# A graph transformer layer pair on one core: edges in 105 chunks instead of 106, with each border chosen in a scan

## The chip, the cores and the metric

The kernel runs on one core of one Trainium2 chip. A core has TensorE (PE in the profile, with its weight loads as PEld), VectorE (DVE), ScalarE (ACT), GpSimd (POOL) and SyncE (SP), each with its own queue of instructions, and 16 DMA engines that all queues share. The metric is the time on the device in microseconds (us) of one execution; lower is better.

## The reference, cut to what matters

There are 6250 nodes with 128 features and 106250 directed edges, sorted by destination. Two transformer convolutions with two heads follow one another; between them stand a batch normalisation and a ReLU, and behind them a residual and a layer normalisation. The edge features are 64 given numbers and 32 cosines of a time difference.

```python
def _transformer_conv(h, edge_attr, src, dst, Wq, bq, Wk, bk, Wv, bv, We, Ws, bs):
    n = h.shape[0]
    C = Wq.shape[1] // H
    q = (h @ Wq + bq).reshape(n, H, C)
    k = (h @ Wk + bk).reshape(n, H, C)
    v = (h @ Wv + bv).reshape(n, H, C)
    e = (edge_attr @ We).reshape(-1, H, C)
    kj = k[src] + e
    alpha = jnp.einsum('ehc,ehc->eh', q[dst], kj) / jnp.sqrt(jnp.asarray(C, h.dtype))
    amax = jax.lax.stop_gradient(jax.ops.segment_max(alpha, dst, num_segments=n))
    ex = jnp.exp(alpha - amax[dst])
    den = jax.ops.segment_sum(ex, dst, num_segments=n)
    a = ex / den[dst]
    out = jax.ops.segment_sum((v[src] + e) * a[:, :, None], dst, num_segments=n)
    return out.reshape(n, H * C) + h @ Ws + bs
...
h = _transformer_conv(x, edge_attr, src, dst, Wq1, bq1, Wk1, bk1, Wv1, bv1, We1, Ws1, bs1)
mu = h.mean(axis=0)
var = ((h - mu) ** 2).mean(axis=0)
h = (h - mu) / jnp.sqrt(var + 1e-05) * bn_g + bn_b
h = jax.nn.relu(h)
return _transformer_conv(h, edge_attr, src, dst, Wq2, bq2, Wk2, bk2, Wv2, bv2, We2, Ws2, bs2)
...
x = _layernorm(x + _L0_gnn_ref(...), axis=-1, eps=1e-05)
```

The sum over a destination's edges runs over neighbouring edges, since the destinations are sorted. So a chunk of edges that begins at a node's first edge and ends behind a node's last edge can be worked on alone.

## The kernel before

**Chunks.** The edges are cut into `NC` = 106 chunks (L48). Each chunk has room for `CE` = 1024 edges (8 columns of 128) and for `NN` = 64 nodes, whose two heads fill 128 rows. A chunk always works on 1024 edges from its first edge on; edges that belong to the next chunk's nodes are masked out by a code of bits for each node.

**The plan ahead of the layers** (`tile_gnn_resnorm`, from L1154). The borders depend on the data, so the kernel works them out on the core. A border is wanted about every `step` = 1003 edges. For each of the 105 inner borders a window of 128 destinations is loaded (`win`, L1157 to L1160). The window's last destination is the border's node; counting how often it stands in the window (`cnt`, L1208) gives that node's first edge (`first`, L1210). A matmul with ones (L1217) turns the 105 rows into one row with all the nodes and one with all the edges (`both`). From it come `slots`, the first edge of each chunk capped at E - 1024 (L1222), and `at` (L1227), by which three indirect DMAs on POOL load the chunks' sources, destinations and weights as rows (L1231). Then `ends`, `nbs` and `sls` hold the borders for the layers (L1235 to L1237). Some small operations check that no chunk has over 64 nodes or 1024 edges, that two neighbouring chunks span no more than 127 nodes, and that the data is sorted (L1246 to L1257 and L1286 to L1291). The result is `oki` (L1310). With `oki` = 1 the path `ordered` runs, and otherwise a general path that makes no use of the order (L1316 to L1319).

Between these steps, in an order written out by hand, the plan also copies the features and times into the table `xv_d` that the first layer gathers from (`pass_features`, L525 to L532), multiplies the weight matrices together (`matrices`), makes the first block of the table of queries (`tables`, L629 to L635), and turns the loaded rows into columns (`columns`, L1268 to L1275).

**The layers** (`conv`, L701, run twice). The loop runs over rounds k from -4 to `NC` + 2. In round k, chunk k + 4 is fetched (SP loads, and 8 gathers of 128 rows each on POOL, L751), chunk k + 1 is turned by PE (L805) and copied by ACT (L812), chunk k is scored (L830, L831) and put through the exponential, chunk k - 1's weights are turned (L855) and its sums gathered (L862), and chunk k - 2 is divided (`fa`, L870), multiplied with the value matrices and finished. All of it is one order written by hand, and each engine takes its part in that order. In the rounds one step of other work is pulled as well (two in the first four rounds and after round 96): in the first layer the tables of the later blocks and then the passing of finished rows, in the second the tables of the second layer. In the second layer finished chunks are normalised in groups whose starts are `STARTS` (L59), the last groups being short.

In the first layer the cosines of the first 43 chunks are taken one chunk at a time, those of later chunks two at a time (`encode` and `sine`, L760 to L784).

Of the kernel before, what the change touches and what calls it, by code (L numbers as in the profile page):

```python
# [7 lines left out]
F32 = mybir.dt.float32  # L8
I32 = mybir.dt.int32
AF = mybir.ActivationFunctionType  # L10
OP = mybir.AluOpType
AX = mybir.AxisListType

P = 128
# [30 lines left out]
T = 8  # L45
CE = T * P
NN = P // H
NC = 106  # L48
EW = ED + 1

BITS = 8
EC = ED + 2 * BITS
# [3 lines left out]
HIGHEST = 2.0 ** 119  # L56

LG = 10
STARTS = (*range(0, 91, LG), 97, 101, 103, 104, 105)  # L59


@with_exitstack
# [472 lines left out]
def room(nc, pl, const, c, w, brief=None):  # L535
# [9 lines left out]

    return ((wq, w["Wq"]), (wk, w["Wk"]), (web[P - EW:P - 1], w["We"]), (bq, w["bq"].rearrange("(p a) -> p a", a=1)),
            (bk, w["bk"].rearrange("(p a) -> p a", a=1)), (web[P - 1:], w["bv"].rearrange("(a d) -> a d", a=1)),
# [28 lines left out]
def matrices(nc, pl, c, const, bank, brief=None):  # L576
# [3 lines left out]
    for i, w in enumerate((wq, wk, web)):  # L580
# [5 lines left out]
        else:  # L586
            nc.vector.memset(t, 0.0)
            nc.vector.tensor_copy(t[:, :ED], pt[:, P - EW:P - 1])
            nc.vector.tensor_copy(t[:, ED:EW], bk)
        turned.append(t)  # L590
# [72 lines left out]
def ordered(ctx: ExitStack, tc: tile.TileContext, pl, x, dst, edge_attr_64, conv2, bn_g, bn_b, out):  # L663
# [16 lines left out]

    enc_d = dram.tile([NC, P, T * TD], F32, name="enc_d")
    et_d = dram.tile([NC, EC, CE], F32, name="et_d")
    xT = pl.xT = const.tile([P, NP], F32, name="fxT")
# [3 lines left out]
    def first(k):  # L687
        return max(0, N - NN * (NC - k)), min(N - 1 if k == NC - 1 else N - NN, NN * k)

# [11 lines left out]
    def conv(c, extra, first_blocks=None):  # L701
# [20 lines left out]
        def fetch(k):  # L722
# [7 lines left out]
            if c:  # L730
                nc.vector.memset(f[:, :, D + EW:1 + D + EW], 1.0)
            else:
                bits = small.tile([P, T, BITS], I32, name="fbits")
                nc.vector.tensor_tensor(bits, pl.dsts[:, :, k:k + 1].to_broadcast([P, T, BITS]),
                                        pl.bitm[:, None, :].to_broadcast([P, T, BITS]), OP.bitwise_and)
                nc.vector.tensor_scalar(f[:, :, D + EW:D + EW + BITS], bits, 0.0, None, op0=OP.is_equal)
                nc.vector.tensor_copy(f[:, :, D + EW + BITS:], bits)
            s.tab = load.tile([P, NN * H, 3 - c], F32, name="ftab")
# [162 lines left out]
        def finish(k):  # L901
# [10 lines left out]

            k0 = max(i for i in STARTS if i <= k)
            g = k - k0
            n = next(i for i in (*STARTS, NC) if i > k) - k0
            if g == 0:
# [17 lines left out]
        def store(j, at, rows, scale):  # L934
            o = small.tile([NN, D], F32, name="fout")
            nc.scalar.activation(o, rows, AF.Copy, scale=scale)
            if j < NC - 1:
                nc.sync.dma_start(out[bass.ds(at, NN), :], o)
            if j > NC - 3:
                nc.sync.dma_start(tail_d[bass.ds(at - base, NN), :], o)  # L940
# [199 lines left out]
def tile_gnn_resnorm(ctx: ExitStack, tc: tile.TileContext, x, src, dst, edge_attr_64, edge_weight, node_vec,  # L1140
                     time_w, time_b, conv1, conv2, bn_g, bn_b, out):
    nc = tc.nc
    N = x.shape[0]
    E = src.shape[0]
    step = -(-E // NC)
# [4 lines left out]
    nbs = keep.tile([1, NC], I32, name="nbs")  # L1150
# [3 lines left out]
    with tc.tile_pool(name="plan", bufs=1) as pl, tc.tile_pool(name="planw", bufs=2) as mw, \  # L1154
            tc.tile_pool(name="planp", bufs=2, space=bass.MemoryType.PSUM) as pp, tc.manual_schedule():
        R = NC - 1
        win = pl.tile([R, P], I32, name="win")  # L1157
        for r0, r1 in ((0, R // 16 * 16), (R // 16 * 16, R)):
            nc.sync.dma_start(win[r0:r1], bass.AP(tensor=dst.tensor, offset=dst.offset + step * (r0 + 1) - (P - 1),
                                                  ap=[[step, r1 - r0], [1, P]]))  # L1160
        NP = got.NP = -(-(N + NN) // GE) * GE
        got.hT = keep.tile([P, NP], F32, name="fhT")
# [21 lines left out]
        tau_i = pl.tile([P, 1], I32, name="tau_i")  # L1184
# [5 lines left out]
        nxt = pl.tile([P, NC], F32, name="nxt")  # L1190
# [3 lines left out]
        ends = pl.tile([1, 2, NC + 1], F32, name="ends")  # L1194
# [9 lines left out]
        winf = pl.tile([R, P], F32, name="winf")  # L1204
        nc.vector.tensor_copy(winf, win)
        eqw = pl.tile([R, P], F32, name="eqw")
        cnt = pl.tile([R, 1], F32, name="cnt")
        nc.vector.tensor_scalar(eqw, winf, winf[:, P - 1:], None, op0=OP.is_equal, op1=OP.add, accum_out=cnt)  # L1208
        first = pl.tile([R, 1], F32, name="first")
        nc.vector.tensor_scalar(first, cnt, -1.0, 1.0, op0=OP.mult, op1=OP.add)  # L1210
        nc.vector.tensor_add(first, first, tau_i[:R])

        vals = pl.tile([R, 2, NC], F32, name="vals")
        nc.vector.tensor_scalar(vals[:, 0], nxt[:R], winf[:, P - 1:], None, op0=OP.mult)
        nc.vector.tensor_scalar(vals[:, 1], nxt[:R], first, None, op0=OP.mult)
        both = pp.tile([P, 2, NC], F32, name="both", tag="fpx")
        nc.tensor.matmul(both, ones[:R], vals, start=True, stop=True)  # L1217

        NR = -(-NC // 16) * 16
        slots = pl.tile([1, NR], F32, name="slots")  # L1220
        nc.vector.memset(slots, 0.0)
        nc.vector.tensor_scalar(slots[:, :NC], both[0:1, 1], float(E - CE), None, op0=OP.min)  # L1222

        pi = pp.tile([P, 1], F32, name="pi", tag="one", bufs=1)
        at = pl.tile([P, 1], I32, name="at")
# [3 lines left out]
        for flat, dtype in ((src, I32), (dst, I32), (edge_weight, F32)):  # L1229
# [2 lines left out]
                out=t.rearrange("c t p -> c (t p)"), out_offset=None, in_=flat.rearrange("(e a) -> e a", a=1),  # L1232
                in_offset=bass.IndirectOffsetOnAxis(ap=at[:NR], axis=0))
            flats.append(t)
        nc.vector.tensor_copy(nbs, both[0:1, 0])  # L1235
        nc.vector.tensor_copy(ends[:, :, :NC], both[0:1])
        nc.vector.tensor_copy(sls, slots[:, :NC])  # L1237

        def bank():
# [46 lines left out]
        nc.vector.tensor_tensor(down, alld[:, 1:ww], alld[:, :ww - 1], OP.is_lt)  # L1286
        worst = pl.tile([P, 1], F32, name="worst")
        nc.vector.tensor_reduce(worst, down, AX.X, OP.add)
        full = pl.tile([R, 1], F32, name="full")
        nc.vector.tensor_scalar(full, cnt, float(P) - 0.5, None, op0=OP.is_gt)  # L1290
        nc.vector.tensor_add(worst[:R], worst[:R], full)  # L1291
        next(passed)
        first_table = tables(nc, got, 0, xT0, 0, mw, wide)
        next(first_table)
# [32 lines left out]
def launch_program(arrays):  # L1327
    import numpy as np
    import concourse.bacc as bacc

    nc = bacc.Bacc("TRN2", target_bir_lowering=False, num_devices=1)
    given, args = {}, {}
    for name, a in arrays.items():
        a = np.ascontiguousarray(a)
        given[f"in_{name}"] = a
        args[name] = nc.dram_tensor(f"in_{name}", a.shape, mybir.dt.from_np(a.dtype), kind="ExternalInput").ap()
    out = nc.dram_tensor("out_0", arrays["x"].shape, F32, kind="ExternalOutput").ap()
    convs = [{w: args[f"{_PRE}{w}{c}"] for w in _WEIGHTS} for c in (1, 2)]
    with tile.TileContext(nc) as tc:
        tile_gnn_resnorm(tc, *(args[n] for n in ("x", "src", "dst", "edge_attr_64", "edge_weight", "node_vec")),  # L1340
                         args[_PRE + "time_w"], args[_PRE + "time_b"], *convs, args[_PRE + "bn_g"],
                         args[_PRE + "bn_b"], out)
    return nc, given
# [7 lines left out]
```

## Time and profile before

| what | value |
|---|---|
| runs of the kernel | 2757.98, 2755.56, 2752.11 us; median 2755.56 |
| the profiled execution's own time | 2730.3 us |
| its span, first to last instruction | 2728.4 us |
| mean granted TensorE clock | 0.952 |
| plan ahead of the layers | about 39 us, to the first gather at 38.71 |
| first layer, first to last `fa` | 125.0 to 1381.8 us |
| second layer, from its second `fa` to its last | 1491.9 to 2715.6 us |

Rows of the groups view read: line, engine and operation, tile written and tiles read, shapes and count, then busy time in us and the mean of one in ns, then the idle time of that engine right before these instructions and what ended it. Rows of the timeline read: start in us, duration in us, engine, line, operation, and in square brackets the idle time before it with what ended it. Rows that show only the `fa` line read: durations min/median/max in ns, then the start of the first and of the last in us. PE's ends are modelled, so its busy share is not a share of its peak.

### The profile page before, as it was taken

To read this page: it belongs to the slowest core of one execution; us is meant where nothing else is said; L and a number is where in the kernel's file an instruction comes from. 1 tells how busy PE (TensorE), PEld (TensorE's weight loads), DVE (VectorE), ACT (ScalarE), POOL (GpSimd) and SP (SyncE) were. 2 spreads that over 40 slices of the span, in tenths; PEclk is the share of its full clock that TensorE was granted. 3 is DMA by queue.
4 is the path that set the end of the run, shared out by engine and by line. 5 is a ranking of instruction groups with operands and counts; after the bars stand their busy time and mean duration, and the time that the engine had idled before them with its cause. 6 is when DMAs were issued, how large, how long until landed. Compare 5 with 4: busy or idle time off the path is not lost. (4 is left out here: it accounts for less than half of the span.)

```text
span 2728.4 us, 39114 instructions
## 1 busy us (share of the span) xinstructions
PE 2340.9 (86%) x11586; PEld 1725.5 (63%) x11586; DVE 1342.3 (49%) x4162; ACT 1241.6 (46%) x2167; POOL 1619.5 (59%) x1717
## 2 busy tenths in 40 slices
PE   5599999999898989888957998888898888888887
PEld 3366666767676767666734665666666666666655
DVE  5366666666666666666634333333333333333333
ACT  2366666665555555445522343333334333333344
POOL 3466666566666666666335666666666666666660
PEclk7799999999999999999978999998999999999998
DMA  6255555545555455555436554555555555544440
GB/s 205 80 177 145 154 164 149 150 131 161 160 151 158 130 163 154 142 150 149 119 106 175 157 154 144 147 156 155 152 153 142 159 151 152 156 135 129 137 135 27
DMA packets 241161, 396.59 MB, mean 145 GB/s; under 512 B 62609, under 2 KB 158094, under 8 KB 237614
## 3 DMA queue, kind: packets, MB, share of 16 engines
q1 hardware_dynamic: 167728, 239.73, 29.5%
q0 software_dynamic: 54656, 113.07, 16.2%
q10 hardware_dynamic: 18558, 41.20, 4.3%
q8 instruction: 98, 1.61, 0.2%
q14 instruction: 121, 0.99, 0.1%
HBM read 277.19 MB, written 113.17 MB: 143 GB/s over the span
## 5 line engine op out<-in xcount | busy, mean ns | idle before, releaser
L751 POOL DMA_INDIRECT ff<-xv_d,fsrcs x848 | 810.1, 955 | 512.8 <-issue 213.0
L751 POOL DMA_INDIRECT ff<-hn_d,fsrcs x824 | 782.2, 949 | 458.8 <-issue 208.7
L812 ACT COPY fft<-fpx 128x512 f32<-128x512 f32 x418 | 246.1, 589 | 1150.2 <-remote 439.9
L862 PE MATMUL fpa<-ff,fpt 128*128 128x225 f32 x3392 | 684.2, 354 | 0.6 <-issue 0.6
L862 PEld LDWEIGHTS fpa<-ff,fpt 128*128 128x128 f32 x3392 | 628.6, 190 | 4.8 <-issue 1.3
L830 PE MATMUL fps<-fft,ftab 128*128 128x512 f32 x848 | 480.4, 650 | 65.5 <-ACT fft L812 45.8
L837 DVE TENSOR_REDUCE flow<-fps 128x1 f32<-128x512 f32 x424 | 285.4, 686 | 455.5 <-PE fpx L805 124.5
L855 PEld LDWEIGHTS fppt<-fident,fs 128*128 128x128 f32 x1696 | 203.4, 145 | 145.2 <-issue 76.4
L856 ACT COPY fpt<-fppt 128x512 f32<-128x512 f32 x424 | 229.4, 585 | 108.8 <-PE fppt L855 47.5
L845 ACT ACTIVATE fs<-fps,fm 128x512 f32<-128x512 f32 x424 | 269.1, 689 | 4.8 <-DVE fm L839 2.1
L805 PE MATMUL fpx<-fident,ff 128*128 128x128 f32 x1696 | 259.3, 276 | 5.3 <-issue 1.1
L830 PEld LDWEIGHTS fps<-fft,ftab 128*128 128x128 f32 x848 | 168.0, 233 | 126.6 <-ACT fft L812 68.2
L855 PE MATMUL fppt<-fident,fs 128*128 128x128 f32 x1696 | 234.6, 282 | 11.6 <-ACT fft L810 5.4
L831 PE MATMUL fps<-fxT,ftab 112*128 112x512 f32 x424 | 236.8, 642 | 2.8 <-DMA fxT<-et_d 2.8
L831 PE MATMUL fps<-fet,ftab 112*128 112x512 f32 x424 | 221.0, 603 | 11.2 <-issue 11.2
L805 PEld LDWEIGHTS fpx<-fident,ff 128*128 128x128 f32 x1696 | 203.4, 142 | 34.8 <-issue 22.7
L817 PE MATMUL fpe<-fident,ff 128*112 128x128 f32 x848 | 133.4, 281 | 72.6 <-ACT fft L812 69.7
L831 PEld LDWEIGHTS fps<-fet,ftab 112*128 112x128 f32 x424 | 106.8, 252 | 91.0 <-issue 88.9
L831 PEld LDWEIGHTS fps<-fxT,ftab 112*128 112x128 f32 x424 | 90.7, 214 | 116.3 <-issue 111.0
L885 DVE COPY fat<-fpo 128x256 f32<-128x256 f32 x212 | 89.2, 421 | 138.9 <-remote 58.9
L817 PEld LDWEIGHTS fpe<-fident,ff 128*112 128x112 f32 x848 | 95.8, 136 | 88.9 <-ACT fft L812 83.3
L818 ACT COPY fet<-fpe 112x512 f32<-112x512 f32 x212 | 127.4, 601 | 45.1 <-remote 16.0
(203 smaller groups left out, 2402.4 us busy)
## 6 DMA issues: line engine op xcount, KB each, us to landing
fmsg<-in_edge_attr SPq DMA_DIRECT2D x212, 256.0 KB
et_d<-fet SPq DMA_DIRECT2D x106, 448.0 KB
fxT<-et_d SPq DMA_DIRECT2D x106, 448.0 KB
ftab<-tab_d SPq DMA_DIRECT2D x106, 192.0 KB
tab_d<-fo ACTq DMA_DIRECT2D x13, 1536.0 KB
ff<-xv_d,fsrcs POOLq DMA_INDIRECT x848
enc_d<-fzs SPq DMA_DIRECT2D x106, 128.0 KB
ftab<-tab_d SPq DMA_DIRECT2D x106, 128.0 KB
```

The source lines that it names most:

```text
L751: nc.gpsimd.indirect_dma_start(out=f[:, t, (1 if c else 0):1 + D], out_offset=None, in_=(h_d if k < RAW else hn_d) if c else pl.xv_d, in_o ...
L805: turn = nc.tensor.transpose(px[:, t * P:(t + 1) * P], s.f[:, u * 4 + t, 1:1 + D], ident)
L812: nc.scalar.copy(s.ft[:, u * GE:(u + 1) * GE], px)
L817: nc.tensor.transpose(pe[:EC, t * P:(t + 1) * P], s.f[:, u * 4 + t, 1 + D:], ident)
L818: nc.scalar.copy(s.et[:, u * GE:(u + 1) * GE], pe[:EC])
L830: nc.tensor.matmul(ps, s.tab[:, :, 0], s.ft[:, w], start=True, stop=False)
L831: nc.tensor.matmul(ps, s.tab[:EC, :, 1], s.et[:, w], start=False, stop=True)
L837: nc.vector.tensor_reduce(low[:, u:u + 1], s.ps[u], AX.X, OP.min)
L845: nc.scalar.activation(s.s[:, u * GE:(u + 1) * GE], s.ps[u], AF.Exp, bias=s.bias, scale=-1.0)
L855: nc.tensor.transpose(pp[:, t * P:(t + 1) * P], s.s[:, at:at + P], ident)
L856: nc.scalar.copy(s.pt[:, u * GE:(u + 1) * GE], pp)
L862: nc.tensor.matmul(s.pa, s.pt[:, t * P:(t + 1) * P], s.f[:, t, 1:1 + D + EW], start=t == 0, stop=t == T - 1)
```

## The change

`NC` becomes 105, so a border is wanted every 1012 edges. The window of 128 destinations now lies around the border's place (`MID` = 63 in front). Two counts replace the one: how often the middle destination stands at or in front of the middle, and how often at or behind it. The first gives the node's first edge (`down_`), the second the next node's first edge (`up`). Of these two places one is taken for each border, in order: the later one (`up`) where the chunk that ends there still has no more than 1024 edges and 64 nodes, and otherwise the earlier one. Whether it does depends on how the border before was chosen, so there are two answers for each border, and a scan along the row (`tensor_tensor_scan`) carries the choice from one to the next (`later`). The chosen edge and node then go where the one place went before, and the check on the windows looks at both counts.

```diff
-NC = 106
+NC = 105
 EW = ED + 1
+MID = P // 2 - 1
...
-STARTS = (*range(0, 91, LG), 97, 101, 103, 104, 105)
+STARTS = (*range(0, 91, LG), 96, 100, 102, 103, 104)
...
-            nc.sync.dma_start(win[r0:r1], bass.AP(tensor=dst.tensor, offset=dst.offset + step * (r0 + 1) - (P - 1),
+            nc.sync.dma_start(win[r0:r1], bass.AP(tensor=dst.tensor, offset=dst.offset + step * (r0 + 1) - MID,
...
-        cnt = pl.tile([R, 1], F32, name="cnt")
-        nc.vector.tensor_scalar(eqw, winf, winf[:, P - 1:], None, op0=OP.is_equal, op1=OP.add, accum_out=cnt)
-        first = pl.tile([R, 1], F32, name="first")
-        nc.vector.tensor_scalar(first, cnt, -1.0, 1.0, op0=OP.mult, op1=OP.add)
-        nc.vector.tensor_add(first, first, tau_i[:R])
-
-        vals = pl.tile([R, 2, NC], F32, name="vals")
-        nc.vector.tensor_scalar(vals[:, 0], nxt[:R], winf[:, P - 1:], None, op0=OP.mult)
-        nc.vector.tensor_scalar(vals[:, 1], nxt[:R], first, None, op0=OP.mult)
-        both = pp.tile([P, 2, NC], F32, name="both", tag="fpx")
+        cnt = pl.tile([R, 2], F32, name="cnt")
+        for i, w in enumerate((slice(0, MID + 1), slice(MID, P))):
+            nc.vector.tensor_scalar(eqw[:, w], winf[:, w], winf[:, MID:MID + 1], None, op0=OP.is_equal, op1=OP.add,
+                                    accum_out=cnt[:, i:i + 1])
+        edge = pl.tile([R, 2], F32, name="edge")
+        nc.vector.tensor_scalar(edge[:, 0:1], cnt[:, 0:1], -1.0, 1.0, op0=OP.mult, op1=OP.add)
+        nc.vector.tensor_copy(edge[:, 1:], cnt[:, 1:])
+        nc.vector.tensor_tensor(edge, edge, tau_i[:R].to_broadcast([R, 2]), OP.add)
+
+        vals = pl.tile([R, 3, NC], F32, name="vals")
+        nc.vector.tensor_scalar(vals[:, 0], nxt[:R], edge[:, 0:1], None, op0=OP.mult)
+        nc.vector.tensor_scalar(vals[:, 1], nxt[:R], edge[:, 1:], None, op0=OP.mult)
+        nc.vector.tensor_scalar(vals[:, 2], nxt[:R], winf[:, MID:MID + 1], None, op0=OP.mult)
+        both = pp.tile([P, 3, NC], F32, name="both", tag="fpx")
         nc.tensor.matmul(both, ones[:R], vals, start=True, stop=True)
+
+        cut = pl.tile([1, 3, NC], F32, name="cut")
+        nc.vector.tensor_copy(cut, both[0:1])
+        down_, up, node = (cut[:, i] for i in range(3))
+        reach = pl.tile([1, 2, NC], F32, name="reach")
+        near = pl.tile([1, 2, NC], F32, name="near")
+        nc.vector.memset(reach[:, :, 0:1], 0.0)
+        for i, (since, n) in enumerate(((up, NN), (down_, NN - 1))):
+            nc.vector.scalar_tensor_tensor(reach[:, i, 1:], since[:, :NC - 1], float(CE), up[:, 1:], op0=OP.add,
+                                           op1=OP.is_ge)
+            nc.vector.scalar_tensor_tensor(near[:, i, 1:], node[:, :NC - 1], float(n), node[:, 1:], op0=OP.add,
+                                           op1=OP.is_ge)
+        nc.vector.tensor_mul(reach[:, :, 1:], reach[:, :, 1:], near[:, :, 1:])
+        nc.vector.tensor_sub(reach[:, 0], reach[:, 0], reach[:, 1])
+        later = pl.tile([1, NC], F32, name="later")
+        nc.vector.tensor_tensor_scan(later, reach[:, 0], reach[:, 1], 0.0, OP.mult, OP.add)
+        nc.vector.tensor_sub(up, up, down_)
+        nc.vector.tensor_mul(up, up, later)
+        nc.vector.tensor_add(ends[:, 1, :NC], down_, up)
...
-        nc.vector.tensor_scalar(slots[:, :NC], both[0:1, 1], float(E - CE), None, op0=OP.min)
+        nc.vector.tensor_scalar(slots[:, :NC], ends[:, 1, :NC], float(E - CE), None, op0=OP.min)
...
-        nc.vector.tensor_copy(nbs, both[0:1, 0])
-        nc.vector.tensor_copy(ends[:, :, :NC], both[0:1])
+        nc.vector.tensor_add(ends[:, 0, :NC], node, later)
+        nc.vector.tensor_copy(nbs, ends[:, 0, :NC])
         nc.vector.tensor_copy(sls, slots[:, :NC])
...
-        full = pl.tile([R, 1], F32, name="full")
-        nc.vector.tensor_scalar(full, cnt, float(P) - 0.5, None, op0=OP.is_gt)
-        nc.vector.tensor_add(worst[:R], worst[:R], full)
+        full = pl.tile([R, 2], F32, name="full")
+        most = pl.tile([R, 2], F32, name="most")
+        nc.vector.memset(most[:, 0:1], float(MID + 1))
+        nc.vector.memset(most[:, 1:], float(P - MID))
+        nc.vector.tensor_tensor(full, cnt, most, OP.is_ge)
+        for i in range(2):
+            nc.vector.tensor_add(worst[:R], worst[:R], full[:, i:i + 1])
```

## The prediction

> **What bounds the kernel now.** I read the page's summary first, then the groups of instructions by line, then two views cut by time: the busy time of the engines by stretch, and the instructions that write the tile `fa`, of which there is exactly one per chunk and layer.
>
> ```profile
> PE 2340.9 (86%) x11586; PEld 1725.5 (63%) x11586; DVE 1342.3 (49%) x4162; ACT 1241.6 (46%) x2167; POOL 1619.5 (59%) x1717
> ```
>
> ```profile
> L751 POOL DMA_INDIRECT ff<-xv_d,fsrcs x848 | 810.1, 955 | 512.8 <-issue 213.0 <-PE fpa L862 130.5 <-PE fpx L805 101.4
> L862 PE MATMUL fpa<-ff,fpt 128*128 128x225 f32 x3392 | 684.2, 354 | 0.6 <-issue 0.6
> L812 ACT COPY fft<-fpx 128x512 f32<-128x512 f32 x418 | 246.1, 589 | 1150.2 <-remote 439.9 <-PE fpx L805 340.4 <-PE fpo L899 195.5
> ```
>
> TensorE (PE) is the busiest engine. Of the idle time before ScalarE's largest group (L812), 340.4 + 195.5 us ended at a named PE instruction; the gathers on POOL, when not spaced by issue (213.0 us), waited mostly for PE too. So a chunk is paced by PE first, with POOL (8 gathers x 955 ns and 213.0 / 848 = 0.25 us of issue each, 9.6 us) not far behind. Which of the two it is matters little here, since all their large groups have counts in proportion to chunks: 3392 = 16 x 2 layers x 106, 848 = 8 x 106. A chunk less takes one round from each layer whichever engine sets the pace. The question is what a round is worth:
>
> ```profile
> L870 DVE TENSOR_SCALAR fa<-fpa,finv x72: 452/453/455, 125.0 to 990.2; 128x225 f32<-128x225 f32 x72
> L870 DVE TENSOR_SCALAR fa<-fpa,finv x23: 452/453/455, 1063.9 to 1326.6; 128x225 f32<-128x225 f32 x23
> L870 DVE TENSOR_SCALAR fa<-fpa,finv x7: 452/453/454, 1326.6 to 1381.8; 128x225 f32<-128x225 f32 x7
> L870 DVE TENSOR_SCALAR fa<-fpa,finv x77: 452/453/455, 1491.9 to 2393.7; 128x225 f32<-128x225 f32 x77
> L870 DVE TENSOR_SCALAR fa<-fpa,finv x21: 452/453/454, 2404.9 to 2643.1; 128x225 f32<-128x225 f32 x21
> L870 DVE TENSOR_SCALAR fa<-fpa,finv x7: 452/453/454, 2654.9 to 2715.6; 128x225 f32<-128x225 f32 x7
> ```
>
> Dividing each stretch by its count less one gives 12.19 and 11.94 us a round in the first layer, 11.87 and 11.91 in the second; the last six intervals, where gathers have run out, are 9.20 and 10.12. The other work spread over the rounds (tables of the next blocks, one step a round) is a fixed 84 steps; with two steps in each of the first four rounds it is used up at round 79, so the stretches from 1063.9 and from 2404.9 are rounds without it.
>
> **The change part by part.** *One round less in each layer.* The last groups' starts, the windows' place and the row counts change no instruction's number. The total of table steps, row writes and group ends (15 `STARTS` groups before and after) stays, and so does the fast end of each layer. What goes is a plain round: 11.94 + 11.91 = 23.85 us. In it are its 16 gathers, 7 SP loads and its stores. From chunk 43 the encodings share one sine by pairs: 63 chunks left one alone, 62 leave none, so one ScalarE sine and its table load go too, inside that price. Lower bound: only the end's rounds are saved, 9.20 + 10.12 = 19.32. Upper bound: rounds with table work, 12.19 + 11.91 = 24.1.
>
> *The borders, ahead of the layers.* These rows are all on DVE, except the matmuls (PE), DMA issue (SP) and gather (POOL):
>
> ```profile
> 3.55 0.35 DVE L1208 TENSOR_SCALAR_CACHE_REDUCE eqw<-winf 105x128 f32<-105x128 f32 x1
> 3.82 0.08 DVE L1208 DVE_READ_ACCUMULATOR eqw<-winf 105x1 f32 x1
> 3.94 0.15 DVE L1210 TENSOR_SCALAR first<-cnt 105x1 f32<-105x1 f32 x1
> 4.27 0.27 DVE L1214 TENSOR_SCALAR vals<-nxt,winf 105x106 f32<-105x106 f32 x1
> 4.46 0.27 DVE L1215 TENSOR_SCALAR vals<-nxt,first 105x106 f32<-105x106 f32 x1
> 4.78 1.07 PE L1217 MATMUL both<-vals,pones 105*128 105x212 f32 x2 [4.78 <-DVE vals L1215]
> 5.89 0.26 DVE L1222 TENSOR_SCALAR slots<-both 1x106 f32<-1x106 f32 x1 [1.06 <-PE both L1217]
> 6.77 0.16 DVE L1227 CAST at<-pi 112x1 int32<-112x1 f32 x1 [0.62 <-PE pi L1226]
> 7.02 0.36 DVE L1236 COPY ends<-both 1x212 f32<-1x212 f32 x1
> 7.43 0.36 DVE L1247 TENSOR_TENSOR span<-ends 1x212 f32<-1x212 f32 x1
> 7.82 0.20 DVE L1248 TENSOR_SCALAR span<-span 1x106 f32<-1x106 f32 x1
> 8.64 0.27 DVE L1255 TENSOR_TENSOR two<-ends 1x105 f32<-1x105 f32 x1
> 8.94 0.20 DVE L1256 TENSOR_SCALAR two<-two 1x105 f32<-1x105 f32 x1
> 9.17 0.25 DVE L1257 TENSOR_REDUCE bad<-two 1x1 f32<-1x105 f32 x1
> 10.46 0.34 DVE L525 COPY fxrows<-fnv 128x48 f32<-128x48 f32 x1 [1.03 <-DMA fnv<-in_node_vec]
> 20.53 0.16 DVE L1291 TENSOR_TENSOR worst<-worst,full 105x1 f32<-105x1 f32 x1
> 24.01 2.32 DVE L635 SCALAR_TENSOR_TENSOR fo<-fpx,fb,fcode 128x512 f32<-128x512 f32 x2 [2.46 <-PE fpx L629]
> 26.16 0.69 DVE L1268 CAST rowf<-rows 106x1024 f32<-106x1024 int32 x1
> 29.68 0.14 DVE L1310 TENSOR_SCALAR oki<-tot 1x1 int32<-1x1 f32 x1
> 31.34 0.32 SPq L529 DMA_DIRECT2D xv_d<-fxrows  x1
> 38.71 0.96 POOL L751 DMA_INDIRECT ff<-xv_d,fsrcs  x1 [27.93 <-DVE fbits L734]
> ```
>
> A step's price is the distance from its start to the next one's; a dependent one-partition operation over 105 elements costs 8.94 - 8.64 = 0.30, one over 212 costs 7.82 - 7.43 = 0.39.
> - Ahead of the matmul: the equality is counted twice over half the elements instead of once, 2 x (about 0.13 + 0.12) against 0.39, but with the fixed part I take +0.27; the copy of the second count +0.15; the third `vals` +0.19 (4.46 - 4.27). Together 0.61.
> - The matmul is 315 wide instead of 212: 1.07 x 103 / 212 = 0.52 more.
> - Behind it, until `slots`: the copy of three rows out of PSUM 0.36 x 315 / 212 = 0.54; the one-element fill 0.06; four compares that don't wait for each other, 0.20 each (the distance of the two independent `vals`), 0.80; the product over 208, 0.39; a subtraction 0.30; the scan; a subtraction beside it 0.20; a product and an addition 0.60. No row shows a scan. Its bounds are a tensor-tensor operation over 105 (0.27) and the two-input operation over 512 (2.32 / 2 = 1.16); as it is 105 long I take the near one, 0.30. Together 3.19.
>
> So `at` comes 0.61 + 0.52 + 3.19 = 4.3 us later, near 11.1. Behind it the 212-wide copy out of PSUM (0.36) is replaced by a 105-wide addition (0.27), and DVE would reach L525 at 9.42 (9.17 + 0.25) + 4.3 - 0.1 = 13.6. Before it reached it at 9.42 but stood until 10.46 for a load; that cover of 1.04 is used, so 13.6 - 10.5 = 3.1 us are left. [...]
>
> Queued behind DVE at L525 is everything of the start: the rows for `xv_d`, the key matrices, the first table, L635, L1268, the decision `oki`, then SP's last write of `xv_d` (31.34) and POOL's first gather (38.71). PE's weight transposes wait too, being behind the wider matmul on its queue, but they had stood ready from 6.66 while DVE used them first at 11.83, so DVE is the later. I find no idle DVE stretch in which the 3.1 is made up, so it passes through. POOL's three gathers of `rows` start 4.3 later than 7.22; the first is used at 26.16, which moves by 3.1, so at most 1.2 can be lost there. The wider `full` test is two fills and two tiny operations more, 4 x 0.16 = 0.64 at most; it lies ahead of L635's wait of 2.46 for PE, and is free as long as that wait stands. From both sides: nothing (a load was late anyway, the writes then run into a free DMA queue) up to 6.9 (13 operations at 0.39, the scan at 1.16 and 0.52 for the matmul, 6.75, less the cover of 1.04, and the 1.2 of the gathers). I take 3.1, which is nearest to the rows.
>
> Sum: -23.85 + 3.1 = -20.75 us. The profiled execution took 2730.3 us and would take 2709.6. The median of the runs, 2755.56, stands 25 us above it, or 0.12 us a round over 212 rounds, which changes the worth of two rounds by 0.24 us; I leave that out: 2755.56 - 20.75 = 2734.8.
>
> **The rivals.** *Only end rounds go.* If POOL's and PE's backlogs are such that the shorter loop loses its cheap rounds, the gain is 19.32 - 6.9 = 12.4 at the least: 2743. Against it: the end's six intervals exist as long as gathers run out, with 105 as with 106.
>
> *A slower granted clock (slower).* The first layer ran at the full granted clock, the second not:
>
> ```profile
> 1060.00:1340.00 280.00, 250.36 (x1320) 195.49 (x1318) 184.81 (x554) 138.92 (x224) 176.55 (x184) 1.00 0.51 146
> 2400.00:2640.00 240.00, 203.80 (x1019) 146.52 (x1018) 81.70 (x286) 90.21 (x196) 152.54 (x162) 0.94 0.46 132
> ```
>
> The columns are span, busy time of PE, PEld, DVE, ACT and POOL, granted clock, DMA share, GB/s. If the moved start puts the first layer at 0.96 as well, its 1257 us (125.0 to 1381.8) would cost up to 4% more, 50 us: 2755.6 - 20.8 + 50 = 2785. It decides from 20.75 / 1257 = 1.7% on. For it: executions of one program differ by 25 us as said. Against it: the second layer at 0.94 has the same round (11.91) as the first at 1.00 (11.94), so the clock is not proportional to time. [...]
>
> *Pace.* A round 0.1 us longer throughout, for no work of its own, would give back 21 us over 210 rounds: about 2756, the same. Nothing in a round's instructions changes, but executions of before already differ by that much.
>
> *The change doesn't do what it says.* The limits are 64 nodes and 1024 edges a chunk. With 105 chunks a border stands every 1012 edges, which leaves 12 to spare where 1003 left 21. If one chunk is over, `oki` is 0 and the general path runs, whose 850 scatters of records alone take 850 x (0.95 + 0.25) = 1020 us before its layers begin, far beyond 3000 us in all. I counted the destinations of the reference's inputs by the new rule: the largest chunk holds 64 nodes and 1024 edges, both exactly allowed, and two neighbours span at most 126 nodes where 127 are allowed. It passes, without a spare edge.
>
> **How the numbers follow.** Plain rounds saved and 1 to 5 us lost ahead: 0.74. Cheap rounds only, or a start near its upper bound: 0.11, still faster. Pace given back: 0.05. Clock: 0.08. General path: 0.02. A measurement here tells some 0.2%, 5.5 us, from no change. Faster 0.85, same 0.05, slower 0.10. The likeliest alone: 19.32 - 5 to 24.1 - 0, 2731 to 2741; with the runs' spread of 2752.11 to 2757.98 about the median and half of the pace rival, the range is 2722 to 2750.
>
> **What would show it.** After: 210 executions of the `fa` line, still 11.8 to 12.0 us apart without tables; 1680 gathers instead of 1696; `at` near 11.1, the first gather of features near 41.8, the first `fa` near 128; `oki` still leading to the same loops. It is wrong if the rounds' distance moves by 0.1 us, if the granted clock of the first layer falls below 0.98, or if the first gather starts more than 7 us later.

## The result, and the profile after

The changed kernel took 2727.74 us (median of four runs, 2719.93 to 2731.63) where the kernel before took 2755.32: a ratio of 0.9896, with a 95% interval from 0.9879 to 0.9913. Worked out on 2755.32 that is 28.7 us less, between 24.0 and 33.3. The forecast was 20.75 less, 2734.8 us. Two later comparisons of the same two kernels gave 0.9908 (0.9890 to 0.9925) and 0.9922 (0.9902 to 0.9942), so 25.3 and 21.6 us less. The medians themselves differ by 27.6, 25.8 and 24.2 us.

The first profile page's line of engines, for the kernel after, and its two groups of gathers:

```profile
PE 2315.9 (85%) x11482; PEld 1703.1 (62%) x11482; DVE 1332.0 (49%) x4144; ACT 1231.3 (45%) x2147; POOL 1608.2 (59%) x1701
...
L752 POOL DMA_INDIRECT ff<-xv_d,fsrcs x840 | 804.8, 958 | 511.9 <-issue 212.4
L752 POOL DMA_INDIRECT ff<-hn_d,fsrcs x816 | 775.8, 951 | 466.0 <-issue 208.0
```

The gathers are 16 fewer (with the 24 from `h_d`, 1680). PE lost 104 matmuls and 25.0 us of busy time; two rounds at PE's busy shares in the stretches of the prediction, 0.89 of 11.94 and 0.85 of 11.91, are 20.8 us. The start is told by the timeline of DVE and POOL in the kernel after:

```profile
3.35 0.28 DVE L1210 TENSOR_SCALAR_CACHE_REDUCE eqw<-winf 104x64 f32<-104x64 f32 x1
...
6.61 0.47 DVE L1225 COPY cut<-both 1x315 f32<-1x315 f32 x1 [1.51 <-PE both L1222]
7.03 0.06 DVE L1229 MEMSET reach<- 1x2 f32 x1
7.12 0.26 DVE L1231 SCALAR_TENSOR_TENSOR reach<-cut 1x104 f32<-1x104 f32 x1
7.30 0.25 DVE L1233 SCALAR_TENSOR_TENSOR near<-cut 1x104 f32<-1x104 f32 x1
7.48 0.25 DVE L1231 SCALAR_TENSOR_TENSOR reach<-cut 1x104 f32<-1x104 f32 x1
7.65 0.25 DVE L1233 SCALAR_TENSOR_TENSOR near<-cut 1x104 f32<-1x104 f32 x1
7.94 0.36 DVE L1235 TENSOR_TENSOR reach<-reach,near 1x208 f32<-1x208 f32 x1
8.34 0.26 DVE L1236 TENSOR_TENSOR reach<-reach 1x105 f32<-1x105 f32 x1
8.63 0.37 DVE L1238 TENSOR_TENSOR_SCAN later<-reach 1x105 f32<-1x105 f32 x1
8.92 0.23 DVE L1239 TENSOR_TENSOR cut<-cut 1x105 f32<-1x105 f32 x1
9.19 0.26 DVE L1240 TENSOR_TENSOR cut<-cut,later 1x105 f32<-1x105 f32 x1
...
10.71 0.16 DVE L1251 CAST at<-pi 112x1 int32<-112x1 f32 x1 [0.62 <-PE pi L1250]
...
13.29 0.22 DVE L526 COPY fxrows<-fnv 128x48 f32<-128x48 f32 x1
...
32.20 0.14 DVE L1338 TENSOR_SCALAR oki<-tot 1x1 int32<-1x1 f32 x1
...
40.53 0.96 POOL L752 DMA_INDIRECT ff<-xv_d,fsrcs  x1 [25.40 <-PE fpx L654]
```

`at` stands at 10.71 where it stood at 6.77, 3.94 later (4.3 was worked out). The copy at L526 no longer waits for a load and starts at 13.29, 2.83 later than before (3.1 was worked out). `oki` is 2.52 later and the first gather 1.82 later.

The rows of the tile `fa` (start of the first and of the last, in us) and the stretches by engine, again after:

```profile
L871 DVE TENSOR_SCALAR fa<-fpa,finv x105: 452/453/455, 129.6 to 1380.4; 128x225 f32<-128x225 f32 x105
L871 DVE TENSOR_SCALAR fa<-fpa,finv x105: 452/453/455, 1478.2 to 2712.9; 128x225 f32<-128x225 f32 x105
```

```profile
1060.00:1340.00 280.00, 248.43 (x1296) 191.17 (x1295) 185.30 (x553) 139.01 (x223) 173.59 (x181) 1.00 0.50 149
2400.00:2640.00 240.00, 204.86 (x1012) 147.77 (x1012) 82.38 (x289) 89.55 (x197) 152.08 (x161) 0.94 0.45 133
```

Where no tables are made, the distances of `fa` are 11.97 us in the first layer (1063.6 to 1338.8, 23 intervals) and 12.00 in the second (2401.2 to 2641.1, 20), against 11.94 and 11.91 before. The granted clock (third number from the end) is 1.00 and 0.94, as before. The two traces differ by only 2.9 us of span (2725.5 against 2728.4), while the runs differ by 28. The trace after was one of its four runs; the trace before, at 2730.3 us, lay 22 us below the lowest of its own runs. So this pair can't say where 28 us went; a second trace of the kernel before was needed.

### The profile page after: what moved, and what is told of

Read it like the earlier page. It is cut to its first block, busy times and chain, and to the rows that moved or that the text cites. A ratio compares the mean times of both kernels' runs of the same rounds, so it can differ in the third digit from the quotient of the medians.

```text
span 2725.5 us, 38782 instructions
## 1 busy us (share of the span) xinstructions
PE 2315.9 (85%) x11482; PEld 1703.1 (62%) x11482; DVE 1332.0 (49%) x4144; ACT 1231.3 (45%) x2147; POOL 1608.2 (59%) x1701
## 3 DMA queue, kind: packets, MB, share of 16 engines
q8 instruction: 97, 1.59, 0.2%
## 5 line engine op out<-in xcount | busy, mean ns | idle before, releaser
L863 PE MATMUL fpa<-ff,fpt 128*128 128x225 f32 x3360 | 677.4, 354 | 3.5 <-issue 3.5
L863 PEld LDWEIGHTS fpa<-ff,fpt 128*128 128x128 f32 x3360 | 621.6, 190 | 8.0 <-issue 4.7
L831 PE MATMUL fps<-fft,ftab 128*128 128x512 f32 x840 | 473.5, 647 | 46.3 <-ACT fft L813 34.5
L832 PE MATMUL fps<-fxT,ftab 112*128 112x512 f32 x420 | 230.8, 632 | 2.5 <-DMA fxT<-et_d 2.5
L806 PEld LDWEIGHTS fpx<-fident,ff 128*128 128x128 f32 x1680 | 200.6, 142 | 40.5 <-issue 27.6
```

The costliest lines, as they stand in the source:

```text
L806: turn = nc.tensor.transpose(px[:, t * P:(t + 1) * P], s.f[:, u * 4 + t, 1:1 + D], ident)
L831: nc.tensor.matmul(ps, s.tab[:, :, 0], s.ft[:, w], start=True, stop=False)
L832: nc.tensor.matmul(ps, s.tab[:EC, :, 1], s.et[:, w], start=False, stop=True)
L863: nc.tensor.matmul(s.pa, s.pt[:, t * P:(t + 1) * P], s.f[:, t, 1:1 + D + EW], start=t == 0, stop=t == T - 1)
```

## The experiments

Each of the three sets of runs shared runs of the kernel before on one chip. The first set ran on a chip on which the kernel before takes 2308 us, the other two on chips on which it takes 2753 and 2764 us. Differences are therefore taken within a set; us are the ratio's distance from 1 times the set's median of before. The chip of the first set is called the fast chip below, the others slow chips.

**The kernel before, unchanged (first set).** No edit.

> The kernel before, unchanged, for a second trace. The profiled execution of before (2730.3 us) lies 25 us below its runs' median. If that one execution was unusual, this trace shows a longer distance between the fa rows, about 12.0 to 12.1 us in both layers, and a span near 2750. If the profile itself makes executions shorter, it shows about 11.9 again and a span near 2728 while the runs stay at 2755.

Measured: 2308.55 us against 2308.07, ratio 0.9999 (0.9990 to 1.0008). Neither theory had thought of a chip on which the same program is 16% faster. The profiled execution took 2311.35 us and so was not short here. The trace is used below as the base of this set.

**The new borders with 106 chunks.** From the changed kernel:

```diff
-NC = 105
+NC = 106
-STARTS = (*range(0, 91, LG), 96, 100, 102, 103, 104)
+STARTS = (*range(0, 91, LG), 97, 101, 103, 104, 105)
```

> The new borders, but with the old 106 chunks: the price ahead of the layers alone. My theory: 3.1 us more than before, ratio 1.001, with the first gather 2 to 3 us later. Rival: the later start shifts the pace of the rounds and gains several us, ratio 0.997 or less, which would explain why the change gained 28 us instead of 21.

Measured: ratio 1.0018 (1.0009 to 1.0026), 4.2 us more (2.1 to 6.0); by the medians, 2311.47 against 2308.07, 3.4 more. The first row here is the base of the set, the second this kernel:

```profile
L870 DVE TENSOR_SCALAR fa<-fpa,finv x106: 452/453/455, 89.3 to 1185.8; 128x225 f32<-128x225 f32 x106
```

```profile
L871 DVE TENSOR_SCALAR fa<-fpa,finv x106: 452/453/457, 92.4 to 1188.1; 128x225 f32<-128x225 f32 x106
```

The first layer starts 3.1 us later and runs as long as before (1095.7 against 1096.5). The first gather came 2.0 us later (40.37 against 38.34), as expected. So on this chip the price of the borders passes through, and the rival, a later start that helps the rounds, is out.

**105 chunks with the old borders.** From the kernel before:

```diff
-NC = 106
+NC = 105
-STARTS = (*range(0, 91, LG), 97, 101, 103, 104, 105)
+STARTS = (*range(0, 91, LG), 96, 100, 102, 103, 104)
-        nc.vector.tensor_scalar(span[:, 1], span[:, 1], float(CE), None, op0=OP.is_gt)
+        nc.vector.tensor_scalar(span[:, 1], span[:, 1], float(CE + 64), None, op0=OP.is_gt)
```

> 105 chunks with the old borders; five chunks have up to 7 edges too many, the limit in the check is loosened by 64 so that the same path runs, and those few edges are left out of the result; the work per chunk is the same. My theory: two plain rounds less, 23.9 us, ratio 0.9913. Rival (a round is worth more, or the rounds' pace changes with the count): 30 us or more, ratio 0.989 or less.

Measured: 0.9914 (0.9899 to 0.9928), 19.8 us less (16.6 to 23.3). The ratio is what I expected, but the us belong to this chip. The base's stretches of rounds without table work:

```profile
L870 DVE TENSOR_SCALAR fa<-fpa,finv x24: 452/453/455, 901.7 to 1133.3; 128x225 f32<-128x225 f32 x24
L870 DVE TENSOR_SCALAR fa<-fpa,finv x23: 452/453/454, 2021.1 to 2239.1; 128x225 f32<-128x225 f32 x23
```

231.6 / 23 + 218.0 / 22 = 10.07 + 9.91 = 19.98 us for a plain round of each layer: what was saved, within 0.2. The first layer's stretch isn't quite bare: finished rows are passed in these rounds (in the first trace of the kernel before, 11 copies into `fhr`, 1085.4 to 1312.6), so a bare round there is worth a little less than 10.07.

**107 chunks with the old borders.**

```diff
-NC = 106
+NC = 107
-STARTS = (*range(0, 91, LG), 97, 101, 103, 104, 105)
+STARTS = (*range(0, 91, LG), 98, 102, 104, 105, 106)
```

> 107 chunks with the old borders: the same step the other way. My theory: two plain rounds more, 23.9 us, ratio 1.0087. If the step from 106 to 105 gained more than a round each because something about 106 is unlucky, this one costs clearly less than the step from 106 to 105 gains; if a round is worth 14 us, it costs 28.

Measured: 1.0090 (1.0077 to 1.0103), 20.8 us more. A step up costs what a step down saves; nothing about 106 is unlucky.

**The changed kernel again (second set, before 2753.17 us).** No edit.

> The changed kernel as it is. On the chip of the runs before this one, 105 chunks alone gave 20.2 us less and the borders alone 3.4 us more. If the two parts simply add (my theory), the changed kernel is 16.8 us below the kernel before there, or about 20.8 where a round takes 11.9 us. If they act on each other (rival: the later start helps the rounds), it is 28 us or more below, as in the first comparison.

Measured: 2727.4 us, ratio 0.9908 (0.9890 to 0.9925), 25.3 us less (20.6 to 30.3). The expectation of 20.8 is just inside, the rival's 28 is inside too; this run alone doesn't decide.

**105 chunks with the old borders, beside it.** The edit is that of the first set.

> 105 chunks with the old borders again (up to 7 edges of five chunks are left out of the result), beside the changed kernel on one chip. My theory: the difference between the two is the price of the borders, 3 to 3.5 us, this one the faster. Rival: this one is not faster.

Measured: 2726.48 us, 0.9901 (0.9882 to 0.9921), 27.3 us less (21.8 to 32.5). It is 0.9 us faster than the changed kernel where 3 to 3.5 was expected; with medians that are sure to some 5 us the sign can't be told. What it does show is that the gain comes with the count of chunks: the old borders with 105 have it too.

**The scan's chain done four times.** From the changed kernel:

```diff
+        for _ in range(4):
-        for i, (since, n) in enumerate(((up, NN), (down_, NN - 1))):
+            for i, (since, n) in enumerate(((up, NN), (down_, NN - 1))):
...
-        nc.vector.tensor_tensor_scan(later, reach[:, 0], reach[:, 1], 0.0, OP.mult, OP.add)
+            nc.vector.tensor_tensor_scan(later, reach[:, 0], reach[:, 1], 0.0, OP.mult, OP.add)
```

> The changed kernel with its four compares, product, subtraction and scan done four times over with the same result. In the trace one such pass takes 1.80 us from 7.12 to 8.92, so at comes 5.4 us later. My theory, that the start passes through to the end: 5.4 us more than the changed kernel. Rival, that some slack later on takes it up: less than 2 us more.

Measured: 2733.51 us, 6.1 more than the changed kernel's 2727.4; ratio to before 0.9933 (0.9917 to 0.9950). The timeline of this kernel has the four scans 1.91 us apart:

```profile
8.68 0.37 DVE L1239 TENSOR_TENSOR_SCAN later<-reach 1x105 f32<-1x105 f32 x1
10.59 0.37 DVE L1239 TENSOR_TENSOR_SCAN later<-reach 1x105 f32<-1x105 f32 x1
12.50 0.37 DVE L1239 TENSOR_TENSOR_SCAN later<-reach 1x105 f32<-1x105 f32 x1
14.42 0.37 DVE L1239 TENSOR_TENSOR_SCAN later<-reach 1x105 f32<-1x105 f32 x1
...
16.51 0.16 DVE L1252 CAST at<-pi 112x1 int32<-112x1 f32 x1 [0.62 <-PE pi L1251]
```

and its first `fa` is 5.3 us later than in the changed kernel on the same chip (133.6 against 128.3):

```profile
L871 DVE TENSOR_SCALAR fa<-fpa,finv x105: 452/453/455, 133.6 to 1383.4; 128x225 f32<-128x225 f32 x105
```

```profile
L871 DVE TENSOR_SCALAR fa<-fpa,finv x105: 452/453/455, 128.3 to 1377.8; 128x225 f32<-128x225 f32 x105
```

The copy at L526 is 5.6 later as well (19.09 against 13.47), and so is the last `fa` of the first layer. The two traced executions end alike all the same (spans 2726.7 and 2726.8): this one was the fastest of its six runs, the other the slowest of its five. That the delay reaches the end rests on the runs: five of the six are above every run of the changed kernel there, although the intervals of the two ratios overlap slightly.

**The checks moved behind the third copy of features.** From the changed kernel, eight operations moved (the expectation says seven):

```diff
-        span = pl.tile([1, 2, NC], F32, name="span")
-        nc.vector.tensor_sub(span, ends[:, :, 1:], ends[:, :, :NC])
...
-        nc.vector.tensor_reduce(bad[:, 2:3], two, AX.X, OP.add)
...
         next(passed)
+        span = pl.tile([1, 2, NC], F32, name="span")
+        nc.vector.tensor_sub(span, ends[:, :, 1:], ends[:, :, :NC])
...
+        nc.vector.tensor_reduce(bad[:, 2:3], two, AX.X, OP.add)
         first_table = tables(nc, got, 0, xT0, 0, mw, wide)
```

> The changed kernel with the checks on the borders (seven operations, 2.0 us from 11.33 to 13.29) moved behind the third copy of features, where VectorE waits 1.9 us for PE. My theory: the start comes 1.5 to 2.0 us earlier and so does the end. Rival, that the start is not set by VectorE there: no difference.

Measured: 2728.92 us against 2727.4 of the changed kernel, ratio to before 0.9912 (0.9895 to 0.9930). In its trace the copy at L526 does start earlier, 11.50 where the changed kernel on this chip has 13.47, and so does the first gather:

```profile
38.83 0.96 POOL L752 DMA_INDIRECT ff<-xv_d,fsrcs  x1 [23.71 <-DMA fwv<-in_L_gnn_Wv]
```

That is 2.1 us earlier than the 40.92 there, and the first `fa` is 1.3 earlier (127.0 against 128.3). No gain shows in the time, and with medians sure to some 5 us a gain of 2 would not. It is inconclusive.

**The changed kernel a third time, and the kernel before beside it (third set, before 2763.85 us).** No edits.

> The changed kernel once more. Comparisons so far fell on chips that differ by a fifth in time: before took 2308 us on one and 2753 us on another. My theory, two plain rounds less and 3.4 us for the borders: 16.8 us below before if before takes 2308 here, 21 if it takes 2753. Rival, something beside the rounds gains too: 25 us or more on either.

> The kernel before once more, for a trace beside the changed kernel's on one chip. If the chip is the slow one, my theory has this profiled execution near 2753 us with fa rows about 12.1 us apart, so that the first trace (2730.3 us) was a short execution and a round is worth 0.1 us more than I took; the rival is 2730 again, with the profile shortening what it measures.

Measured: 0.9922 (0.9902 to 0.9942), 21.6 us less (16.0 to 27.1), for the changed kernel, near the theory's 21, though the rival's 25 lies in the interval too. The kernel before was 1.0003 of itself, and its profiled execution took 2753.89 us, the theory's side: a profiled execution is not always 2730, and the first trace was a short one. This one was again the fastest of its twelve, 10.6 us below their median, and the borders alone below have one 11.8 under theirs, while most traces lie within 2 us of their medians. Whether profiling shortens some executions stays open. The rows of the kernel before, and then of the changed one, on this chip:

```profile
L870 DVE TENSOR_SCALAR fa<-fpa,finv x106: 452/453/455, 126.0 to 1390.7; 128x225 f32<-128x225 f32 x106
L870 DVE TENSOR_SCALAR fa<-fpa,finv x106: 452/453/457, 1488.3 to 2739.4; 128x225 f32<-128x225 f32 x106
```

```profile
L871 DVE TENSOR_SCALAR fa<-fpa,finv x105: 452/453/456, 126.8 to 1386.2; 128x225 f32<-128x225 f32 x105
L871 DVE TENSOR_SCALAR fa<-fpa,finv x105: 452/453/456, 1484.0 to 2724.6; 128x225 f32<-128x225 f32 x105
```

Divided by one less than their counts: 12.04 and 11.92 us a round before, 12.11 and 11.93 after. Over whole layers a round is worth 23.96 us for both together. It did not get shorter by the change, and the trace does not show it getting longer by more than executions differ: in the first trace of the unchanged kernel it was 11.97 (1256.8 / 105) and 11.78 (1236.6 / 105).

**The borders alone, and 107 chunks, on this chip.** The edits are those of the first set.

> The borders alone, with 106 chunks, a second time. Theory: 3 to 3.5 us more than before on any chip, since the start does not depend on the rounds. Rival: on the slow chip nothing, or a gain.

Measured: 1.0011 (0.9994 to 1.0028), 3.0 us more by the ratio and 0.9 by the medians, from 1.7 less to 7.7 more. It fits the theory, but no cost at all fits it too.

> 107 chunks, old borders, a second time. Theory: two plain rounds more, 20 to 22 us where before takes 2308 and 24 us where it takes 2753. Rival: the step from 106 to 105 is larger than the one from 107 to 106, so this one costs under 20 us on the slow chip.

Measured: 1.0087 (1.0065 to 1.0110), 24.0 us more (18.0 to 30.4): the two rounds of this chip, 23.96. The rival, under 20 us, isn't excluded by the interval.

## Why the prediction was right

**A round less in each layer** was the term that decides, and it held in three ways: 105 chunks alone gave 19.8 us where two plain rounds are 19.98, 107 chunks alone cost 24.0 where they are 23.96, and 105 alone on the second set's chip gave 27.3, with an interval (21.8 to 32.5) that holds 23.85. That plain rounds go and not the end's was argued from the loop, and 19.32 lies outside the interval of the last of these and inside that of the 107 chunks. The traces say it more plainly, for the cheap rounds of the end are still there. In the trace after, the last six intervals of the first layer take 8.75 us each (9.20 before) and the last seven of the second 10.26 (10.36 before):

```profile
L871 DVE TENSOR_SCALAR fa<-fpa,finv x7: 452/452/454, 1327.9 to 1380.4; 128x225 f32<-128x225 f32 x7
L871 DVE TENSOR_SCALAR fa<-fpa,finv x8: 452/453/454, 2641.1 to 2712.9; 128x225 f32<-128x225 f32 x8
```

The reading of the price was a little off: the prediction takes the first layer's stretch from 1063.9 to hold no other work, but the trace before has 11 copies into `fhr` in it (1085.4 to 1312.6), the passing of finished rows. The first layer has no bare stretch, and its 11.94 holds about half a pass. No run shows what that is worth.

**The borders**: 3.1 us were taken, and 4.2 (2.1 to 6.0) were measured on the one chip where zero lies outside the interval, 3.0 with a wide interval on a slow one. Of the parts, the estimates by distances of starts came out near: the wider matmul took 1.42 (1.07 + 0.52 = 1.59 worked out), the copy of three rows a distance of 0.42 (0.54), the scan 0.29 (0.30), and altogether `at` 3.94 (4.3). The windows had landed 0.2 sooner in the trace after; from the start of the counting (3.55 before, 3.35 after) to `at` it is 4.14 more. The scan lasted 0.37 us where the product over as many elements, L1240, lasted 0.26, which is 0.11 more for 105 elements; the product over 208 elements (L1235) lasted 0.36, about as long as the scan over half as many. Why the scan lasts longer, no run shows. The 0.11 is on the path too: the subtraction at L1239 does not depend on the scan, yet began 0.29 after it, where the four compares, which don't wait for each other, began 0.18 apart. In the run with four chains the operation behind each of the first three scans began 0.40 after it.

One step was put too simply: that no idle stretch makes up for the delay. In the first pair `oki` is 2.52 later and the first gather only 1.82, so 0.7 us was made up between the two; of the 2.83 that DVE had lost at L526, 0.3 had gone before `oki`. The cover also varies: the old kernel's wait for the load at L525 was 1.03 in this pair and 0.69 in its trace on the fast chip (10.10 us), where L526 came 3.34 later with the borders alone (13.44). Over all traces, those with four chains and with late checks aside, the first gather stands at 36.88 to 38.71 in the seven with the old borders and at 39.76 to 40.92 in the five with the new ones, 2.4 later on average. The first `fa` was then 4.6 later in the first pair, 3.1 on the fast chip, and 0.8 (changed kernel) and 1.7 (borders alone) in the third set. On slow chips the way from the first gather to the first `fa`, 86 to 89 us (38.71 to 125.0 before, 40.53 to 129.6 after), differs between executions by about as much as the borders cost.

**The size** was on the low side: 28.7, 25.3 and 21.6 against 20.75. The interval of the first comparison leaves 20.75 out, those of the other two hold it. One reason that I can name is small: the trace from which the round's price was read was a short execution, and the whole layers' mean was 11.97 + 11.78 = 23.75 there and 23.96 in the trace at 2753.89, 0.2 us. No run shows a gain beside the rounds: the borders alone never gained in time, and 105 chunks with the old borders were as fast as the change. But scatter alone is a poor reading. All three comparisons lie above the forecast; their mean is 25.2, and if their intervals are independent it is sure to about 3 us, which leaves 20.75 out. Part of it may be that the borders cost less on slow chips: the two comparisons of medians there gave 0.9 us each (2727.4 against 2726.48, 2764.79 against 2763.85), sure to some 5 us only. Rounds of 23.96 less 0.9 would be 23.1, an estimate, inside the intervals of the second and third comparison and 0.9 below that of the first. So the mechanism held, but one or both terms of the sum were off by some us, and which one isn't settled.

**The rivals.** The slower clock did not come: 1.00 and 0.94 in the same stretches after as before. The pace of a round in the first pair moved by 0.06 and 0.09 us in the two layers (12.03 and 11.87 against 11.97 and 11.78), less than the 0.07 and 0.14 between the two slow-chip traces of the kernel before. The general path did not run; the gathers' counts are those of the layers.

## What to carry to other kernels

Where every large group of instructions has a count in proportion to the chunks, a chunk less was worth one ordinary round of the loop, on the fast chip, where PE was busy 962 of the 970 us from 130 to 1100 us, as on slow ones, where it was busy 877 to 882 of them. Read the round's price as the distance of one instruction that occurs once a chunk, in a stretch without side work, and look in the trace whether the stretch really has none. Small operations at the start cost their distance from start to start, minus the first wait that they cover: here 0.27 to 0.30 us for one over 105 elements that needs the result before it, and 0.18 for one that doesn't. Before reading a pair of traces against each other, see where each one lies among its kernel's own runs: here the unchanged kernel's first trace was 25 us short, nearly the whole gain, and parts tried alone, both up and down, showed where the gain comes from.

## What the runs showed of the hardware

The same program took 2308 us on one chip and 2753 to 2764 us on others. It isn't the granted clock alone: in the stretch from 130 to 1100 us it was 1.00 on the fast chip and 0.99 on the slow one of the third set, but PE was busy 962 and 877 of 970 us. The kernel before on the fast chip, and then on the slow one:

```profile
130.00:1100.00 970.00, 962.39 (x5127) 777.97 (x5126) 721.96 (x2172) 651.76 (x965) 720.74 (x744) 1.00 0.61 175
```

```profile
130.00:1100.00 970.00, 877.48 (x4403) 661.82 (x4402) 617.77 (x1863) 567.87 (x850) 606.89 (x633) 0.99 0.51 152
```

In the groups by line, ScalarE's copy behind PE's transposes waits twice as long on the slow chip (1180.6 against 588.3 us), and 430.0 of it ended at what the profile calls `remote`, with no instruction named; on the fast chip nearly all waits end at PE's instruction. Fast first, then slow:

```profile
L812 ACT COPY fft<-fpx 128x512 f32<-128x512 f32 x418 | 244.6, 585 | 588.3 <-PE fpx L805 579.5 <-PE fpo L883 5.4 <-PE fpa L862 3.3
```

```profile
L812 ACT COPY fft<-fpx 128x512 f32<-128x512 f32 x418 | 246.5, 590 | 1180.6 <-remote 430.0 <-PE fpx L805 295.2 <-PE fpo L899 279.6
```

The durations of the copies are alike (585 and 590 ns); it is the waits that differ. PE's ends are modelled in these profiles, so PE may have been slower there than its rows say.

By the first `fa` the slow chip has lost 37 us (89.3 on the fast chip, 126.0 on the slow one), and none of it ahead of the first gather, which stands at 38.34 and 36.88. From 40 to 130 us PE was busy for 72.6 to 74.8 us at a granted clock of 0.87 to 0.89 in the four traces from the fast chip, and for 37.1 to 42.6 us at 0.62 to 0.67 in eight of the ten from slow chips. In the first trace of the kernel before, ScalarE begins three copies there after 9.90, 10.61 and 20.77 us of idle time that ended at nothing named, although by PE's modelled rows the matmuls that they read had ended 14 us before or earlier:

```profile
73.28 0.59 ACT L812 COPY fft<-fpx 128x512 f32<-128x512 f32 x1 [9.90 <-remote]
84.48 0.59 ACT L818 COPY fet<-fpe 112x512 f32<-112x512 f32 x1 [10.61 <-remote]
106.25 0.59 ACT L812 COPY fft<-fpx 128x512 f32<-128x512 f32 x1 [20.77 <-remote]
```

PE finishing later than its rows say would look like this, and so would ScalarE being held by something that the profile doesn't show; no run decides between them.
